# Graph attention layer: the edges' node numbers kept on chip and spread over the partitions by TensorE

## The chip, the cores and the metric

The kernel runs on one core of a Trainium2 chip. The metric is the device time of one execution in microseconds (us). All times here come from runs on the chip, or from the trace of one profiled execution.

## The reference

One layer of a graph network with a layer norm ahead of it and a residual around it: 12,500 nodes of 128 features, 200,000 edges, sorted by the node `dst` that they end in. What is computed, shortened:

```python
h = relu(layernorm(x))                       # (12500, 128)
Q, K = h @ W_Q.T, h @ W_K.T
score = einsum('md,md->m', Q[dst], K[src]) / sqrt(128) * exp(-edge_weight)   # per edge
# per node dst: keep the 16 best scores, softmax over them -> alpha (0 for the other edges)
agg = segment_sum(alpha[:, None] * (h[src] @ W_msg.T), dst)
out = x + relu(h @ W_self.T + agg)
```

## The kernel before

**Tiling.** The edges are cut into chunks of 128 (one edge per partition) and the chunks into G = 112 groups of GC = 14. Since edges are sorted, a group's edges end in some 112 consecutive nodes; a group also looks at the first chunk of the next (NJ = 15 chunks), so that its nodes are complete. W_Q and W_K are folded into one matrix `a_qk`, so the score of an edge is (h[dst] a_qk) . h[src].

**Prologue.** x is loaded in seven pieces on SyncE's (SP's) queue, normalised on ScalarE (`normed`, L214) and written to the table `h_tab` in device memory. `src`, `dst` and `edge_weight` are loaded as rows of 13 chunks (`load_rows`, on ScalarE's queue) and turned into columns by TensorE transposes (`to_columns`): the indices of the gathers (`idx_all`), each edge's rank within its node (`pos_all`), its decay (`dec_all`) and its node, from which `dlw` (the node's place relative to the group's first node) is made. `gather` (L172) fetches the rows of 128 edges with one indirect DMA, issued by GpSimd (POOL); a group has 14 of these. The first RAW = 4 groups are gathered straight from x, before `h_tab` is there, and normalised afterwards (`raw_stats`, `raw_normed`); groups 4 to 6 are gathered from `h_tab` all at once behind them. Their rows lie in `hs`, a ring of seven groups.

**The main loop** (the listing's `for i in range(-3, G + 6)`) is a software pipeline written out by hand: the order of the calls is each engine's order of instructions (`tc.manual_schedule()`), and one iteration holds stages of different groups. For a group, in the order of its data:

- `load_dst` brings `dst` of 15 x 128 edges, the same row to all 128 partitions, into `dstb` (960 KB over SP's queue). `far_of` (L522) takes the square of its distance from the partition's node in one ScalarE pass of 128x1920, `to_edges` (L527) makes a 0/1 matrix `to_e` (node by edge) of it. `places` (L533, L535) makes two small 0/1 tables.
- `q_to_edges` (L546), in four parts b = 0 to 3, spreads q of the nodes over the edges with `to_e`: three bf16 products per chunk. `scores` (L556) multiplies with the gathered rows on VectorE (DVE).
- `scores_in_slots` (L564), `slots_by_node` (L569, L571: 30 products) and `slots_out`, `node_by_slots` bring the scores of a node together in 40 slots; `best` (L585 to L597) finds the 16 best on VectorE: `ell` is its first result, `km` its last. `sum_of_exps` (L602) is on ScalarE.
- `kept_to_edges` (L614, 15 products) brings the verdict back to the edges; `on_edges` (L620 to L627), `exps` (L631) and `weights` (L635, L636) make the weights `alz`.
- `sums` (L646), in two parts of seven and eight chunks, adds up the weighted rows in PSUM. `sums_out` (L651) writes them to `agn`, `sums_turned` (L654) transposes, `sums_turned_out` (L658) copies to `aggT`, `products` (L661, L662), `output` (L666) and `store` finish the group.

`let_go(g, k)`, called as `more(k)` at seven places of an iteration, copies two columns of indices (L472, on VectorE) and issues two gathers of a later group: POOL waits for the copy, and for the `hs` buffer of seven groups earlier to be free, which `sums` has read last. In one iteration the calls `more(0)` to `more(4)` and `more(5)`, `more(6)` belong to two groups.

PSUM has eight banks of 128 x 512 words; `bank(tag, bufs)` hands them out. The sums have one, tag `a`, with a single buffer:

```python
            if part == 0:
                T[g]["pa"] = bank("a", 1)
```

Of the kernel before, what the change touches and what calls it, by code (L numbers as in the profile page):

```python
# [41 lines left out]
RAW = 4  # L42
# [34 lines left out]
def gnn_layer(  # L77
# [38 lines left out]
    CPR = 13  # L116
# [4 lines left out]
    assert RR <= P and RR - RF <= 1  # L121
# [22 lines left out]
    nvec = const.tile([P, 1], F32, name="nvec")  # L144
    a_qk = const.tile([P, P], F32, name="a_qk")
# [8 lines left out]
    nb = const.tile([P, G], F32, name="nb")  # L154
# [79 lines left out]
    with tc.tile_pool(name="edges", bufs=1) as ep, ExitStack() as stage:  # L234
        prep = stage.enter_context(tc.tile_pool(name="prep", bufs=1))
        RL = HALO + RW

        src_r = ep.tile([RR, RL], I32, name="src_r")
        h0 = src_r.bitcast(F32)
        h1 = alz[0][0:RR, 0:RL]  # L240
        dst_all = alz[1][:, 0:CW]
        assert max(RL, CW) <= NJ * (WW + STEP)
        dst_r = ep.tile([RR, HALO + RW], I32, name="dst_r")
# [24 lines left out]
        nc.vector.memset(src_r, 0)  # L268
        load_rows(src_r, src)
        xs, t = [], 0  # L270
        for i, n in enumerate(sizes):
# [12 lines left out]
        nc.vector.memset(ew_r, 0.0)  # L284
# [10 lines left out]
        nc.vector.memset(dst_all[:, RR * CPR:CW], float(1 << 21))  # L295
# [13 lines left out]
        def finish(i):  # L309
            t0, n, xg = xs[i]  # L310
            normed(xg, n, *stat[i])
            if i == 1:
                for t, w in zip(ws, (w_q, w_k, w_self, w_msg)):
                    nc.scalar.dma_start(t, w)
                nc.scalar.dma_start(b_i[:, 1:G],
                                    bass.AP(dst.tensor, dst.offset + EG - 1, [[EG, 1], [EG, G - 1]]))

# [10 lines left out]
            if i == 1:  # L328
                load_dst(0)
# [6 lines left out]
        for g in range(RAW, min(7, G)):  # L336
            gather_at_once(g, h_tab)
# [592 lines left out]
```

## Time and profile before

| | us |
|---|---|
| time, median of 9 runs | 2692.22 |
| lowest and highest | 2687.59 and 2698.76 |
| the profiled execution's own time | 2688.1 |
| its span in the trace | 2686.3 |
| first gather of the main loop | 213.63 |
| end of the last gather | 2610.16 |

The mean granted TensorE clock of the profiled execution is 0.691. In the lines of the profile, PE is TensorE's products, PEld its weight loads, DVE VectorE, ACT ScalarE, POOL GpSimd, SP SyncE; L172 is a line of the kernel. A line of the timeline has start and duration in us, then engine, line, operation, output <- inputs, the count, and in brackets the idle time before it and what ended it ("remote": a signal of another engine that the trace can't place; "issue": nothing that the trace shows). A line of the waits has the time waited in all, the number of waits and the longest. Matmuls are pipelined, and their ends in the trace are modelled.

### The profile page before, as it was taken

The numbers are of one execution on the slowest core, as the hardware profiler recorded it, in microseconds if no ns is written. First come the engines' busy times: TensorE is split into PE (matmuls) and PEld (weight loads), VectorE is DVE, ScalarE is ACT, GpSimd is POOL, SyncE is SP. The second block draws the span as 40 slices with busy tenths as digits, with TensorE's granted clock in tenths as the row PEclk, the third lists the DMA queues.
The fourth block names the chain that finished last, engine by engine and source line by source line (L and its number), as shares of the span: only waits on it lengthen the run. The fifth ranks groups of instructions, "written<-read, shape, count | busy, mean of one in ns | idle before, by whom it ended". The sixth has DMA issues, their size and how long they took to land. (4 is left out here: it accounts for less than half of the span.)

```text
span 2686.3 us, 43581 instructions
## 1 busy us (share of the span) xinstructions
PE 1740.9 (65%) x14574; PEld 1484.2 (55%) x14575; DVE 1475.9 (55%) x7420; ACT 648.4 (24%) x1306; POOL 1526.1 (57%) x1578
## 2 busy tenths in 40 slices
PE   0236666666767666766676766766776677766676
PEld 0125555555555655655555655555565566565555
DVE  5547555555555555555555555555555555555555
ACT  5532122222222222222222222222222222222221
POOL 4725555555555665555555555555566655555550
PEclk9657676666666667667666666666667766666668
DMA  8412322333333233322232332332323232222320
GB/s 223 151 57 91 93 94 92 94 94 94 94 94 95 95 95 94 94 90 86 90 94 91 95 94 93 94 94 94 95 95 95 94 94 92 87 89 92 93 81 8
DMA packets 117572, 253.17 MB, mean 94 GB/s; under 512 B 32798, under 2 KB 76065, under 8 KB 116576
## 3 DMA queue, kind: packets, MB, share of 16 engines
q1 hardware_dynamic: 66104, 144.92, 15.6%
q0 software_dynamic: 50144, 102.74, 14.3%
q10 hardware_dynamic: 1094, 2.69, 0.5%
q8 instruction: 115, 1.88, 0.3%
q14 instruction: 115, 0.94, 0.1%
HBM read 236.40 MB, written 14.40 MB: 93 GB/s over the span
## 5 line engine op out<-in xcount | busy, mean ns | idle before, releaser
L172 POOL DMA_INDIRECT hs<-h_tab,ix x1465 | 1415.4, 966 | 1034.0 <-DVE prod L556 492.2
L646 PE MATMUL a<-hs,alz 128*128 128x128 f32 x3348 | 729.3, 384 | 98.3 <-issue 83.6
L646 PEld LDWEIGHTS a<-hs,alz 128*128 128x128 f32 x3348 | 664.3, 290 | 154.6 <-issue 122.9
L546 PE MATMUL q<-q,to_e 128*128 128x128 bf16 x5022 | 545.1, 259 | 281.5 <-issue 232.8
L546 PEld LDWEIGHTS <-to_e 128*128 128x128 bf16 x5022 | 417.1, 115 | 364.0 <-issue 353.3
L556 DVE SCALAR_TENSOR_TENSOR prod<-hs,dec_all,q 128x128 f32<-128x128 f32 x1674 | 483.6, 343 | 68.2 <-remote 31.3
L585 DVE TENSOR_SCALAR ell<-slots,e 128x40 f32<-128x40 f32 x112 | 27.9, 249 | 864.7 <-remote 820.6
L571 PE MATMUL e<-ow,sl 128*41 128x40 f32 x3348 | 248.2, 247 | 50.9 <-issue 46.1
L602 ACT ACTIVATE e<-v,km 128x16 f32<-128x16 f32 x112 | 34.4, 307 | 972.0 <-DVE km L594 957.1
L571 PEld LDWEIGHTS e<-ow,sl 128*41 128x41 f32 x3348 | 216.0, 162 | 74.1 <-issue 57.6
L651 ACT ACTIVATE agn<-a,rden 128x128 f32<-128x128 f32 x112 | 41.2, 368 | 777.8 <-remote 486.5
L654 PE MATMUL s<-ident,agn 128*128 128x128 f32 x112 | 39.1, 349 | 283.9 <-ACT up L631 89.8
L522 ACT ACTIVATE far<-dstb,nb 128x1920 bf16<-128x1920 int32 x112 | 212.9, 1901 | 0.0
L527 ACT ACTIVATE to_e<-far 128x1920 bf16<-128x1920 bf16 x112 | 201.1, 1796 | 0.0
L654 PEld LDWEIGHTS s<-ident,agn 128*128 128x128 f32 x112 | 17.1, 153 | 305.1 <-ACT agn L651 114.5
L556 DVE DVE_READ_ACCUMULATOR prod<-hs,dec_all,q 128x1 f32 x1674 | 137.5, 82 | 0.0
L472 DVE COPY ix<-idx_all 128x2 int32<-128x2 int32 (+1 forms) x733 | 130.6, 178 | 0.0
L614 PE MATMUL x<-km,to_e 128*128 128x43 bf16 x1674 | 78.8, 204 | 43.0 <-DVE km L597 34.0
L614 PEld LDWEIGHTS <-to_e 128*128 128x128 bf16 x1674 | 66.0, 112 | 69.9 <-DVE km L597 61.7
L666 DVE SCALAR_TENSOR_TENSOR o<-s,x_t 128x128 f32<-128x128 f32 x112 | 32.5, 290 | 126.1 <-issue 119.1
L506 PE MATMUL s<-a_qk,hT 128*128 128x128 f32 x224 | 57.4, 339 | 66.8 <-issue 48.2
L564 DVE TENSOR_TENSOR sl<-po,s 128x600 f32<-128x600 f32 x112 | 87.7, 783 | 3.8
(166 smaller groups left out, 1643.3 us busy)
## 6 DMA issues: line engine op xcount, KB each, us to landing
dstb<-in_dst_dram SPq DMA_DIRECT2D x111, 960.0 KB
hs<-h_tab,ix POOLq DMA_INDIRECT x1465
h_r<-h_tab SPq DMA_DIRECT2D x112, 64.0 KB
x_t<-in_x_dram SPq DMA_DIRECT2D x108, 64.0 KB
out_dram<-o SPq DMA_DIRECT2D x108, 64.0 KB
xg<-in_x_dram SPq DMA_DIRECT2D x2, 1400.0 KB
h_tab<-xg SPq DMA_DIRECT2D x2, 1400.0 KB
xg<-in_x_dram SPq DMA_DIRECT2D x1, 1120.0 KB
```

The source lines that it names most:

```text
L172: nc.gpsimd.indirect_dma_start(out=T[g]["hs"][:, j, :], out_offset=None, in_=table[0:N, :], in_offset=bass.IndirectOffsetOnAxis(ap=index(j ...
L472: nc.vector.tensor_copy(ix[:, j0:j1], idx_all[:, GC * g + j0:GC * g + j1])
L506: nc.tensor.matmul(so[:, P:2 * P], lhsT=T[g]["hT"], rhs=a_qk, start=True, stop=True)
L522: nc.scalar.activation(T[g]["far"][:, 0:n], T[g]["dstb"][:, 0:n], AF.Square, bias=nb[:, g:g + 1])
L527: nc.scalar.activation(T[g]["to_e"][:, 0:n], T[g]["far"][:, 0:n], AF.Relu, bias=1.0, scale=-1.0)
L546: nc.tensor.matmul(pq[:, (j - j0) * P:(j - j0 + 1) * P], lhsT=T[g]["to_e"][:, j * P:(j + 1) * P], rhs=upper(T[g]["q"][:, k, :]), start=(k ...
L556: nc.vector.scalar_tensor_tensor(prod, rows_of(g, j), dec_all[:, c:c + 1], T[g]["pq", b][:, (j % 4) * P:(j % 4 + 1) * P], op0=OP.mult, op1 ...
L564: nc.vector.tensor_tensor(sl1[g % 2][:, 0:n, 0:KM], T[g]["po"][:, 0:n, :], bc(T[g]["s"][:, 0:n], KM), op=OP.mult)
L571: nc.tensor.matmul(et[0:KM + 1, STEP * j:STEP * j + WN], lhsT=sl1[g % 2][:, j, :], rhs=T[g]["ow"][:, j, :], start=False, stop=(j == n - 1))
L614: nc.tensor.matmul(px[:, j, 0:KM + 3], lhsT=T[g]["to_e"][:, j * P:(j + 1) * P], rhs=upper(T[g]["km"]), start=True, stop=True)
L646: nc.tensor.matmul(T[g]["pa"][:, 0:P], lhsT=alz[g % 2][:, WW * j + PRE:WW * j + PRE + P], rhs=rows_of(g, j), start=(j == 0), stop=(j == n ...
L654: nc.tensor.transpose(so[:, 2 * P:3 * P], T[g]["agn"], ident)
```

## The change

Rows now hold 14 chunks, one row per group (`CPR = GC`). A constant `rel` (bf16, 112 x 1920) holds for every group, on the group's own partition, the nodes of its 15 chunks minus the group's first node. The broadcast of `dst` (`load_dst`, `dstb`) goes. In its place `far_of(g, b)`, for b = 0 to 3, multiplies `rel` by a column of the identity, broadcast to 128 columns: a product that puts row g of 512 columns (384 in the last part) on all partitions, in the PSUM bank with tag `a`; ScalarE takes the Square from there, with the partition's number as bias. The four calls are put at four places of the iteration. `far` has two buffers instead of one. `dlw` is made by 15 such products with the identity, in place of the transposes of `dst` and three VectorE passes over 128x1680.

`src` is loaded first on SP's queue, ahead of x, and the weights, `dst` and `edge_weight` follow x on the same queue (ScalarE's before). RAW is 3 instead of 4. Groups 3 to 6 are gathered from `h_tab` by `let_go`: group 3 in seven steps between the VectorE instructions of the prologue, groups 4, 5 and 6 in iterations -1, 0 and 1 of the loop. The index copies have a ring of six buffers instead of four. The two `memset` of `alz` go from VectorE to GpSimd.

```diff
--- before.py
+++ after.py
@@ -39,7 +39,7 @@
-RAW = 4
+RAW = 3
@@ -113,12 +113,12 @@
-    CPR = 13
+    CPR = GC
     RW = CPR * P
     REM = M - RF * RW
-    assert RR <= P and RR - RF <= 1
+    assert RR == G and RR <= P and RF > 1 and (REM == 0 or REM >= P)
     CW = GC * (G + 1)
@@ -142,6 +142,9 @@
     nvec = const.tile([P, 1], F32, name="nvec")
+    minus = const.tile([P, 1], F32, name="minus")
+    rel = const.tile([RR, RW + P], BF16, name="rel")
     a_qk = const.tile([P, P], F32, name="a_qk")
...
@@ -176,14 +178,16 @@
-    def load_dst(g):
-        n = chunks[g] * P
-        lo = g * EG
-        T[g]["dstb"] = dstb = rows_pool.tile([P, NJ * P], I32, name="dstb", bufs=2)
-        hi = min(lo + n, M)
-        if hi < lo + n:
-            nc.vector.memset(dstb[:, hi - lo:n], 1 << 21)
-        nc.sync.dma_start(dstb[:, 0:hi - lo], dst[lo:hi].partition_broadcast(P))
+    def let_go(g, k):
+        j0, j1 = 2 * k, min(2 * k + 2, own[g])
+        if j0 >= j1:
+            return
+        if k == 0:
+            T[g]["ix"] = rows_pool.tile([P, GC], I32, name="ix", bufs=6)
+        ix = T[g]["ix"]
+        nc.vector.tensor_copy(ix[:, j0:j1], idx_all[:, GC * g + j0:GC * g + j1])
+        gather(g, j0, j1, lambda j: ix[:, j:j + 1])
...
@@ -248,10 +249,11 @@
         def load_rows(t, a):
-            if RF:
-                nc.scalar.dma_start(t[0:RF, 0:RW], a[0:RF * RW].rearrange("(p c) -> p c", c=RW))
+            nc.sync.dma_start(t[0:RF, 0:RW], a[0:RF * RW].rearrange("(p c) -> p c", c=RW))
             if REM:
-                nc.scalar.dma_start(t[RF:RF + 1, 0:REM], a[RF * RW:M].rearrange("(p c) -> p c", p=1))
+                nc.sync.dma_start(t[RF:RF + 1, 0:REM], a[RF * RW:M].rearrange("(p c) -> p c", p=1))
+                nc.sync.dma_start(t[RF:RF + 1, REM:RW], a[0:RW - REM].rearrange("(p c) -> p c", p=1))
...
@@ -274,14 +275,24 @@
             t += n
+        for t, w in zip(ws, (w_q, w_k, w_self, w_msg)):
+            nc.sync.dma_start(t, w)
+        nc.sync.dma_start(b_i[:, 1:G], bass.AP(dst.tensor, dst.offset + EG - 1, [[EG, 1], [EG, G - 1]]))
         make_identity(nc, ident)
-        nc.gpsimd.iota(dst_r, pattern=[[1, RL]], base=1 << 21, channel_multiplier=0)
+        nc.gpsimd.iota(dst_r, pattern=[[1, RL + P]], base=1 << 21, channel_multiplier=0)
         nc.gpsimd.memset(dst_r[0:1, 0:HALO], -1)
+        nc.sync.dma_start(dst_r[0:1, HALO:], dst[0:RW + P].rearrange("(p c) -> p c", p=1))
+        nc.sync.dma_start(dst_r[1:RF, :] if REM else dst_r[1:RF - 1, :],
+                          bass.AP(dst.tensor, dst.offset + RW - HALO, [[RW, RF - 1 if REM else RF - 2], [1, RL + P]]))
+        k = RF if REM else RF - 1
+        nc.sync.dma_start(dst_r[k:k + 1, 0:HALO + M - k * RW], dst[k * RW - HALO:M].rearrange("(p c) -> p c", p=1))
+        load_rows(ew_r, ew)
         nc.gpsimd.iota(slots, pattern=[[1, KM]], base=0, channel_multiplier=0,
                        allow_small_or_imprecise_dtypes=True)
-        nc.vector.memset(ew_r, 0.0)
+        for k in range(2):
+            nc.gpsimd.memset(alz[k], 0.0)
         nc.vector.memset(ones, 1.0)
...
@@ -309,32 +320,14 @@
             normed(xg, n, *stat[i])
-            if i == 1:
-                for t, w in zip(ws, (w_q, w_k, w_self, w_msg)):
-                    nc.scalar.dma_start(t, w)
-                nc.scalar.dma_start(b_i[:, 1:G],
-                                    bass.AP(dst.tensor, dst.offset + EG - 1, [[EG, 1], [EG, G - 1]]))
-                nc.scalar.dma_start(dst_r[0:1, HALO:], dst[0:RW].rearrange("(p c) -> p c", p=1))
-                if RF > 1:
-                    nc.scalar.dma_start(dst_r[1:RF, :], bass.AP(dst.tensor, dst.offset + RW - HALO,
-                                                                [[RW, RF - 1], [1, RL]]))
-                if REM:
-                    nc.scalar.dma_start(dst_r[RF:RF + 1, 0:HALO + REM],
-                                        dst[RF * RW - HALO:M].rearrange("(p c) -> p c", p=1))
-                load_rows(ew_r, ew)
             for a, b in cuts:
                 nc.sync.dma_start(by_part(h_tab)[a:b, t0:t0 + n, :], xg[a:b])
-            if i == 1:
-                load_dst(0)
                 finish(i)
-        for g in range(RAW, min(7, G)):
-            gather_at_once(g, h_tab)
@@ -354,6 +347,7 @@
         nc.vector.tensor_copy(row_i[:, 1, G - TAIL:G], row[:, 3, 0:TAIL])
+        let_go(RAW, 0)
         pb = bank("s", 1)
@@ -361,22 +355,29 @@
         nc.vector.tensor_copy(dst_f, dst_r)
+        let_go(RAW, 1)
+        nc.vector.tensor_scalar(rel, dst_f[:, HALO:], dst_f[:, HALO - 1:HALO], 1.0, op0=OP.subtract, op1=OP.subtract)
+        let_go(RAW, 2)
         nc.vector.memset(h0[:, 0:1], 0.0)
         nc.vector.tensor_tensor(h0[:, 1:RL], dst_f[:, 1:RL], dst_f[:, 0:RL - 1], op=OP.is_equal)
+        let_go(RAW, 3)
         nc.vector.tensor_tensor_scan(h1, h0, h0, 0.0, op0=OP.mult, op1=OP.add)
+        let_go(RAW, 4)
         bb = rows_pool.tile([P, 2, G], F32, name="bb")
         nc.vector.tensor_copy(bb, pb[:, 0:2 * G].rearrange("p (a g) -> p a g", a=2))
-        nc.vector.tensor_scalar(nb, bb[:, 0, :], nvec, -1.0, op0=OP.add, op1=OP.mult)
-        to_columns(dst_f, HALO, lambda at, p: nc.scalar.copy(at(dst_all), p))
+        for j0 in range(0, NJ, 4):
+            j1 = min(j0 + 4, NJ)
+            pt = bank("q", 3)
+            for j in range(j0, j1):
+                nc.tensor.matmul(pt[:, (j - j0) * RR:(j - j0 + 1) * RR], lhsT=rel[:, j * P:(j + 1) * P],
+                                 rhs=upper(ident[0:RR, 0:RR]), start=True, stop=True)
+            nc.vector.tensor_tensor(dlw.rearrange("e g j -> e j g")[:, j0:j1, :],
+                                    pt[:, 0:(j1 - j0) * RR].rearrange("e (j g) -> e j g", g=RR),
+                                    bc(w0[:, j0:j1], RR), op=OP.subtract)
         to_columns(h1, HALO, lambda at, p: nc.scalar.copy(at(pos_all), p))
         to_columns(ew_r, 0, lambda at, p: nc.scalar.activation(at(dec_all), p, AF.Exp, scale=-1.0))
-        byg = dst_all.rearrange("e (g j) -> e g j", j=GC)
-        nc.vector.tensor_sub(dlw[:, :, 0:GC], byg[:, 0:G, :], bc(bb[:, 0, :], GC))
-        nc.vector.tensor_sub(dlw[:, :, GC], byg[:, 1:G + 1, 0], bb[:, 0, :])
-        nc.vector.tensor_tensor(dlw, dlw, bm(w0, G), op=OP.subtract)
-        for k in range(2):
-            nc.vector.memset(alz[k], 0.0)
+        let_go(RAW, 5)
         nc.vector.scalar_tensor_tensor(h0[:, HALO:RL], dst_f[:, HALO - 1:RL - 1], 0.0, dst_f[:, HALO:RL],
...
@@ -516,10 +507,16 @@
-        def far_of(g):
-            n = chunks[g] * P
-            T[g]["far"] = win.tile([P, NJ * P], BF16, name="far", bufs=1)
-            nc.scalar.activation(T[g]["far"][:, 0:n], T[g]["dstb"][:, 0:n], AF.Square, bias=nb[:, g:g + 1])
+        def far_of(g, b):
+            n0, n1 = 4 * P * b, min(4 * P * (b + 1), chunks[g] * P)
+            if n0 >= n1:
+                return
+            if b == 0:
+                T[g]["far"] = win.tile([P, NJ * P], BF16, name="far")
+            pr = bank("a", 1)
+            nc.tensor.matmul(pr[:, 0:n1 - n0], lhsT=upper(ident[0:RR, g:g + 1]).to_broadcast([RR, P]),
+                             rhs=rel[:, n0:n1], start=True, stop=True)
+            nc.scalar.activation(T[g]["far"][:, n0:n1], pr[:, 0:n1 - n0], AF.Square, bias=minus)
@@ -683,8 +680,6 @@
             at(i + 3, load_nodes)
-            if i + 2 > 0:
-                at(i + 2, load_dst)
             if i == 8:
@@ -694,21 +689,29 @@
-                g, k = (i + 3, k + 2) if k < 5 else (i + 4, k - 5)
-                if 7 <= g < G:
+                if i in (-1, 0, 1):
+                    g = i + 5
+                else:
+                    g, k = (i + 3, k + 2) if k < 5 else (i + 4, k - 5)
+                    if g < 7:
+                        return
+                if i >= -1 and g < G:
                     let_go(g, k)
             at(i, q_to_edges, 0)
+            at(i + 1, far_of, 0)
             at(i - 5, output)
             at(i - 4, sums_turned)
+            at(i + 1, far_of, 1)
             at(i - 4, sums_turned_out)
             at(i, q_to_edges, 1)
-            at(i + 1, far_of)
+            at(i + 1, far_of, 2)
             at(i - 1, slots_by_node)
+            at(i + 1, far_of, 3)
             at(i + 1, places)
                 at(i + 1, raw_normed)
```

More of the change, by code (lines that the diff above doesn't have):

```diff
@@ L152, in gnn_layer @@
     dlw = const.tile([P, G, NJ], F32, name="dlw")
-    nb = const.tile([P, G], F32, name="nb")
     idxo = const.tile([P, TAIL], I32, name="idxo")
@@ L239, in gnn_layer @@
         h0 = src_r.bitcast(F32)
[L240 to L243, printed above, removed]
+        h1 = ep.tile([RR, RL], F32, name="h1")
+        dst_r = ep.tile([RR, RL + P], I32, name="dst_r")
         ew_r = ep.tile([RR, RW], F32, name="ew_r")
@@ L265, in to_columns @@
                     pt[:, 0:(j1 - j0) * RR].rearrange("e (j p) -> e j p", p=RR))
-        nc.vector.memset(src_r, 0)
         load_rows(src_r, src)
@@ L294, in gnn_layer @@
         nc.vector.memset(dec_all[:, RR * CPR:CW], 0.0)
-        nc.vector.memset(dst_all[:, RR * CPR:CW], float(1 << 21))
+        nc.vector.tensor_scalar(minus, nvec, -1.0, None, op0=OP.mult)
         for j in range(NJ):
@@ L390, in gnn_layer @@
         nc.vector.tensor_copy(badc, bad)
+        let_go(RAW, 6)
         t0 = ep.tile([P, TAIL], F32, name="t0")
@@ L462, in rows_of @@
             return T[g]["hs"][:, j, :] if j < GC else T[g + 1]["hs"][:, 0, :]
-        def let_go(g, k):
-            j0, j1 = 2 * k, min(2 * k + 2, own[g])
-            if j0 >= j1:
-                return
-            if k == 0:
-                T[g]["ix"] = win.tile([P, GC], I32, name="ix", bufs=4)
-            ix = T[g]["ix"]
-            nc.vector.tensor_copy(ix[:, j0:j1], idx_all[:, GC * g + j0:GC * g + j1])
-            gather(g, j0, j1, lambda j: ix[:, j:j + 1])
         def start_of(g, row, most):
```

## The prediction, made before the changed kernel was run

> **What bounds the kernel now.** I read the page's shares first, then the groups of instructions by form, the waits, and the timeline of two groups of edges.
>
> The page gives no engine more than 65% of the span:
>
> ```profile
> PE 1740.9 (65%) x14574; PEld 1484.2 (55%) x14575; DVE 1475.9 (55%) x7420; ACT 648.4 (24%) x1306; POOL 1526.1 (57%) x1578
> ...
> q1 hardware_dynamic: 66104, 144.92, 15.6%
> q0 software_dynamic: 50144, 102.74, 14.3%
> ```
>
> So the limit is a cycle of waits, not an engine's work. The waits name it:
>
> ```profile
> DVE ell L585 <- remote: 820.6, 96, 8.7
> POOL hs L172 <- DVE prod L556: 492.2, 208, 52.8
> ACT agn L651 <- remote: 486.5, 69, 7.3
> POOL hs L172 <- remote: 119.0, 71, 1.9
> ```
>
> GpSimd (POOL) issues one gather after another and stops twice per group. The timeline of one group:
>
> ```profile
> 1210.64 0.94 POOL L172 DMA_INDIRECT hs<-h_tab,ix  x1 [0.30 <-issue]
> 1215.67 0.95 POOL L172 DMA_INDIRECT hs<-h_tab,ix  x1 [4.09 <-DVE prod L556]
> 1221.94 0.94 POOL L172 DMA_INDIRECT hs<-h_tab,ix  x1 [0.30 <-issue]
> 1224.58 0.94 POOL L172 DMA_INDIRECT hs<-h_tab,ix  x1 [1.69 <-remote]
> ...
> 1206.01 0.26 PE L571 MATMUL e<-ow,sl 128*41 128x40 f32 x2 [0.45 <-issue]
> 1213.28 0.25 DVE L585 TENSOR_SCALAR ell<-slots,e 128x40 f32<-128x40 f32 x1 [8.70 <-remote]
> 1224.38 0.37 ACT L651 ACTIVATE agn<-a,rden 128x128 f32<-128x128 f32 x1 [7.05 <-remote]
> ```
>
> Eight gathers end at 1211.58. The last L571 matmul is recorded at 1206.01, yet the vector engine's `ell`, which needs it, starts only at 1213.28, 1.7 us after that burst's last gather. Then `best` (about 2 us) and an index copy let POOL go on at 1215.67. Six more gathers end at 1222.89; ScalarE's `agn` starts 1.5 us later, and then POOL. I call these two moments drain 1 and drain 2: what TensorE signals while gathers run reaches the other engines mostly when the burst has landed. So a group is 14 gathers x (0.966 + 0.30) = 17.7 us, plus pauses beyond 0.30 of about 3.8 and 1.4 us: 22.9 us. Without gathers the same group takes little more than half (columns: window, its length, busy time and count of PE, PEld, DVE, ACT, POOL, then granted clock, DMA share, GB/s):
>
> ```profile
> 1202.08:1224.96 22.88, 13.29 (x130) 10.98 (x131) 12.49 (x65) 5.10 (x10) 13.45 (x15) 0.85 0.30 93
> 2617.00:2629.50 12.50, 9.51 (x130) 8.82 (x131) 11.70 (x58) 5.21 (x10) 0.00 (x0) 1.00 0.02 7
> 213.60:2610.20 2396.60, 1641.59 (x13604) 1396.77 (x13602) 1315.20 (x6696) 534.51 (x1047) 1415.37 (x1465) 0.68 0.30 93
> ```
>
> Span: 213.6 (before the loop's first gather) + 2396.6 (1465 gathers, 104.6 groups of 14, 22.9 each) + 76.1 after the last = 2686.3, and 1.8 around it is the profiled 2688.1. The runs' median, 2692.2, is 4 us above it.
>
> **The change, part by part.**
>
> *Removed: the broadcast of dst.* 111 transfers of 960 KB, 544 KB for the last, are some 110 of q1's 144.9 MB. In the timeline they lie beside burst 1; burst 2 has none, and both issue a gather every 1.25 us. In the prologue's burst (108.6 to 160.8 us) only gathers moved, and ScalarE still waited:
>
> ```profile
> 111.62 0.41 PE L499 MATMUL s<-ident,h_r 128*128 128x128 f32 x1
> 159.06 0.27 ACT L503 COPY hT<-s 128x128 f32<-128x128 f32 x1 [41.91 <-remote]
> ```
>
> So the gathers, not this traffic, hold TensorE's signals back. Its worth in the loop: 0. (The Trainium skill, "DMA: Bandwidth & Descriptors", section "Issuing engines are not separate DMA queues", says all issuers share the same 16 engines and interleave. By that, the estimate is 110/144.9 of 15.6% of the span, some 317 us, at most.)
>
> *Prologue.* Sources land first, not behind x, so the first raw gather comes at about 11 us instead of 23.9. 42 raw gathers at 1.5 us (56 took 84.4 us) end near 74, before h_tab is written (81.7). The 42 gathers at once from h_tab go; group 3's 14 are let go from the vector engine's queue, 4 to 6 in iterations -1 to 1 at the loop's own pace. So TensorE isn't held for 42 us, and POOL's wait of 52.8 us before its first loop gather shrinks. With iteration -1 starting near 100 (group 0's first q matmul is at 107.8 now): 100 + three iterations with gathers (22.9) + 1.6 without (12.5) = 189. The early end: the three groups' 42 gathers alone take 42 x 1.27 = 53, which gives 173; all 4.6 at 22.9 give 205. Gain 24.6, between 9 and 41. Moved on queues: weights, dst and weights of edges go from ScalarE's queue to SP's, ahead of the h_tab writes; those wait for normalised rows (from 26 us) anyway, price 0 to 5. POOL's memsets of `alz` come before its first gather, which waits for the sources: 0 to 4, taken as 0. The 15 one-hot products that replace dst's transposes and three big vector passes: -3 to +2, taken as 0.
>
> *Added in the loop.* Per group, four one-hot matmuls of 512, 512, 512 and 384 columns and four Squares from PSUM. Rows of 128 bf16 columns start 0.056 us apart at full clock, 0.107 at half: 0.22 or 0.43 per matmul, under 1.7 in all, beside TensorE's 9.6 idle. Squares: now one of 1.91 (128x1920); in pieces about 0.62 each (a 128-column copy from PSUM, 0.27, plus 384 columns at L522's 1 ns each), 2.5 in all; ScalarE is 24% busy. Both lie in idle time; the work itself costs 0.
>
> *What isn't hidden: the order.* All four products and the sums of group i-3 use the one bank `a`. So each iteration has one closed chain: `agn` (bank free) -> product 0 -> Square 0 -> ... -> product 3 -> Square 3 -> sums part 0. Behind the products' waits stand, in TensorE's queue, L654, q's second part, L571 and q's third part with the sums; behind the Squares, on ScalarE, `aggT` and `q` (wanted an iteration later) and the exponentials of L602 (957 us of waiting in all: cover enough). Product 3 stands behind L571 in TensorE's queue, and L571's signal comes at drain 1. Product 3's likewise. So Square 3 starts at drain 1 at the earliest, and ends some 0.8 us later with its hand-over. Only then can the seven columns of sums part 0 start, of which now half are issued before drain 1. Behind them in TensorE's queue is L614, the kept slots to the edges. At a group whose clock is typical at that moment:
>
> ```profile
> 1488.31 0.25 DVE L585 TENSOR_SCALAR ell<-slots,e 128x40 f32<-128x40 f32 x1 [7.01 <-remote]
> 1490.42 0.73 PE L614 MATMUL x<-km,to_e 128*128 128x43 bf16 x15 [0.56 <-DVE km L597]
> 1490.71 0.95 POOL L172 DMA_INDIRECT hs<-h_tab,ix  x1 [3.66 <-DVE prod L556]
> 1492.47 3.22 PE L646 MATMUL a<-hs,alz 128*128 128x128 f32 x16
> ```
>
> and the granted clock around it (the third number from the end):
>
> ```profile
> 1487.90:1490.90 3.00, 2.23 (x20) 1.84 (x20) 2.38 (x18) 0.94 (x4) 0.19 (x1) 0.50 0.02 5
> ```
>
> L614 starts 2.1 us after `ell`, on `km`, and ends at +2.8, just after POOL's next burst starts (+2.4) and before its gathers land. After: 0.8 + 14 records x 0.20 (3.22/16) = +3.6 to 3.8. Burst 1 slowed TensorE's records about 1.5 us after its first gather (1201.68 to 1203.16), so at +3.9: L614, 15 products long, is caught. Its reader on the vector engine, L620 `on_edges`, runs at +6.2 now, in mid-burst. Caught, it waits for drain 2 (+11.1). Queued behind it on the vector engine is the index copy of `more(5)`, 2.1 us of `on_edges` later, plus 0.3 for the hand-over to POOL: the next burst starts at +13.6 instead of +11.3. Price 2.3 us a group. Bounds: 0 (L614 still in time) and +4 (product 0 also caught behind q's matmuls, Square 2 at drain 1, q's third part, queued behind product 3, late too). I take 2.3, since the clock row says 0.50.
>
> (The Trainium skill, "TensorE: Matmul & The Clock Gate", section "HAM oscillation — how this bites in real kernels", has the clock drop to half after idle windows, which short products separated by ScalarE's waits make likelier. It speaks against this change; warm, the sum would be 14 x 0.11 = 1.6, L614 at +2.4, in time.)
>
> Sum: 189 + 104.6 x 25.2 = 2636, + 78 (76 now, and one group's 2 more) = 2903; + 1.8 = 2905, and + 4 to the median: **2909**.
>
> **The rivals.**
> *Hidden (faster).* L614 is not caught, or Squares 0 to 2 and 3 slip through during burst 1, where TensorE does issue something each 0.7 us. Only the prologue counts: 189 + 2396.6 + 76.1 + 1.8 + 4 = 2667 (2651 to 2682 by its bounds). For it: L620 has 4.9 us of slack before drain 2, and the tail's records are 0.12 apart. Against it: clock 0.50 at drain 1. It decides at L614 ending before about +4. Chance 0.23.
> *Partly caught.* The lateness touches some groups only, 0.3 to 1.5 us on the mean: 2698 to 2824. Chance 0.10.
> *The broadcast did matter.* If it slowed TensorE, the two pauses (5.2 us a group) shrink by 1 to 4: 2250 to 2560. Against it: burst 2 and the prologue's burst. Chance 0.07.
> *Worse.* Product 1 or 2 is itself held to drain 1; then q's second part and L571's 30 products run after it and `ell` slips, by more than 4 us a group: over 3085. Chance 0.10.
>
> **How the numbers follow.** My forecast (1.5 to 4 us a group on 2667, so 2824 to 3085) has 0.50. The range, 2650 to 3085, reaches from the hidden case's early end to the forecast's late one; it leaves out the broadcast case and the worse one, 0.17. A measurement here tells about 0.2% (some 5 us) from no change; the runs spread over 0.4%. Faster: 0.21 of hidden + 0.07 = 0.28; same: 0.03 (hidden, with the prologue's gain lost, or little caught); slower 0.69.
>
> **What would show it.** Right: q1 near 35 MB; first loop gather near 189; `ell` still 1.7 us after burst 1; the last Square after drain 1, sums part 0 after it, L614 at +3.6 or later from `ell`; L620 waiting for drain 2; POOL's second pause 4 us instead of 1.7; period near 25.2. Wrong: L614 still bound by `km` at +2.1 (hidden), `ell` well before drain 1 (the broadcast), or L571's products recorded after it (worse).

## The result, and the profile after

The changed kernel takes 2700.24 us (median of 9 runs, 2698.49 to 2703.87), the kernel before 2691.51 (29 runs): ratio 1.0032, 95% interval 1.0019 to 1.0046. It is slower by 9 us where 217 were forecast; the sign and the range came out right, though not for the reason that the forecast gave, and the size did not. The profiled execution took 2701.8 us, 2700.0 of it span.

The line numbers after the change are lower by three from far_of on (L568 is the old L571, L582 L585, L611 L614, L617 L620, L643 L646, L648 L651); the gathers are at L174, the Squares at L519.

Cut at the loop's first gather and at the end of the last one (window, length, busy time and count of PE, PEld, DVE, ACT, POOL, then clock, DMA share, GB/s), the kernel before:

```profile
0.00:213.63 213.63, 50.67 (x436) 43.11 (x438) 112.18 (x489) 99.00 (x219) 106.00 (x109) 0.76 0.49 141
213.63:2610.16 2396.53, 1641.52 (x13604) 1396.69 (x13602) 1315.13 (x6696) 534.44 (x1046) 1415.37 (x1465) 0.68 0.30 93
2610.16:2686.30 76.14, 48.75 (x540) 44.35 (x539) 48.62 (x237) 14.91 (x43) 4.71 (x5) 0.86 0.03 9
```

and after:

```profile
0.00:207.25 207.25, 59.94 (x466) 46.30 (x468) 103.62 (x492) 95.62 (x216) 102.45 (x112) 0.79 0.41 112
207.25:2618.54 2411.29, 1636.80 (x13993) 1341.97 (x13993) 1314.20 (x6696) 610.38 (x1361) 1438.66 (x1465) 0.74 0.19 50
2618.54:2700.00 81.46, 55.03 (x569) 49.49 (x568) 48.64 (x236) 16.00 (x48) 4.21 (x4) 0.81 0.03 8
```

So the prologue gave 6.4 us (24.6 forecast), the loop cost 14.8 (240 forecast), and the tail 5.3 (2 forecast): 13.7 between the two profiles. The traffic did go; the loop's went from 93 to 50 GB/s, and the queue table has

```profile
q1 hardware_dynamic: 51027, 37.99, 5.0%
```

The waits of the changed kernel (us in all, times, longest):

```profile
DVE ell L582 <- remote: 751.7, 99, 7.7
ACT agn L648 <- remote: 707.8, 98, 7.3
ACT far L519 <- remote: 605.1, 102, 11.9
PEld a L643 <- ACT far L519: 427.8, 102, 5.1
POOL hs L174 <- DVE prod L553: 414.3, 208, 4.2
...
POOL hs L174 <- remote: 176.5, 95, 4.5
```

The third and fourth are the forecast chain: in 100 of 112 groups the last of the four Squares waited for a held signal, and the sums waited for that Square. POOL's two pauses are still the two drains: the first shorter by 0.2 us on the mean (3.62, 3.84 before), the second longer by 0.16 (2.00, 1.84). The timeline of one group:

```profile
1201.54 0.94 POOL L174 DMA_INDIRECT hs<-h_tab,ix  x1 [1.90 <-remote]
...
1204.04 1.44 POOL L174 DMA_INDIRECT hs<-h_tab,ix  x1 [0.30 <-issue]
...
1213.07 0.25 DVE L582 TENSOR_SCALAR ell<-slots,e 128x40 f32<-128x40 f32 x1 [7.61 <-remote]
1213.11 0.58 ACT L519 ACTIVATE far<-a,minus 128x384 bf16<-128x384 f32 x1 [5.83 <-remote]
1213.74 3.35 PE L643 MATMUL a<-hs,alz 128*128 128x128 f32 x14 [3.83 <-ACT far L519]
...
1215.46 0.94 POOL L174 DMA_INDIRECT hs<-h_tab,ix  x1 [3.75 <-DVE prod L553]
...
1216.89 0.76 PE L611 MATMUL x<-km,to_e 128*128 128x43 bf16 x15
...
1219.67 0.20 DVE L617 TENSOR_REDUCE up<-x 128x15 f32<-128x45 f32 x1 [0.33 <-PE a L643]
...
1224.30 0.37 ACT L648 ACTIVATE agn<-a,rden 128x128 f32<-128x128 f32 x1 [7.18 <-remote]
1224.49 0.94 POOL L174 DMA_INDIRECT hs<-h_tab,ix  x1 [1.81 <-remote]
```

The last Square starts at drain 1, the sums 0.67 after `ell` and not half before it, L611 at +3.82 instead of +2.1: the forecast within 0.15 us. But `on_edges` (L617) runs at +6.60, in mid-burst, not at +11. L611 was let through. In the kernel before, for the group whose `ell` is at 1213.28, `on_edges` was at +6.19:

```profile
1219.47 0.20 DVE L620 TENSOR_REDUCE up<-x 128x15 f32<-128x45 f32 x1
```

### The profile page after: what moved, and what is told of

The parts are those of the page before. It is cut to its first block, busy times and chain, and to the rows that moved or that the text cites. A ratio compares the mean times of both kernels' runs of the same rounds, so it can differ in the third digit from the quotient of the medians.

```text
span 2700.0 us, 44305 instructions
## 1 busy us (share of the span) xinstructions
PE 1751.8 (65%) x15026; PEld 1437.8 (53%) x15027; DVE 1466.5 (54%) x7422; ACT 722.0 (27%) x1622; POOL 1545.3 (57%) x1580
## 3 DMA queue, kind: packets, MB, share of 16 engines
q0 software_dynamic: 50144, 102.74, 14.5%
## 5 line engine op out<-in xcount | busy, mean ns | idle before, releaser
L174 POOL DMA_INDIRECT hs<-h_tab,ix x1521 | 1494.4, 983 | 1047.6 <-DVE prod L553 414.3
L643 PE MATMUL a<-hs,alz 128*128 128x128 f32 x3348 | 601.1, 351 | 413.2 <-ACT far L519 406.7
L643 PEld LDWEIGHTS a<-hs,alz 128*128 128x128 f32 x3348 | 557.7, 259 | 435.2 <-ACT far L519 427.8
L543 PEld LDWEIGHTS <-to_e 128*128 128x128 bf16 x5022 | 432.6, 119 | 393.9 <-issue 386.1
L519 ACT ACTIVATE far<-a,minus 128x512 bf16<-128x512 f32 (+1 forms) x447 | 294.9, 660 | 970.4 <-remote 605.1
L582 DVE TENSOR_SCALAR ell<-slots,e 128x40 f32<-128x40 f32 x112 | 27.9, 249 | 796.7 <-remote 751.7
L517 PE MATMUL a<-rel,ident 112*128 112x512 bf16 (+1 forms) x447 | 231.9, 519 | 73.7 <-ACT far L519 26.7
L648 ACT ACTIVATE agn<-a,rden 128x128 f32<-128x128 f32 x112 | 41.1, 367 | 782.3 <-remote 707.8
L568 PE MATMUL e<-ow,sl 128*41 128x40 f32 x3348 | 237.2, 257 | 0.2 <-DVE sl L561 0.2
L568 PEld LDWEIGHTS e<-ow,sl 128*41 128x41 f32 x3348 | 222.1, 175 | 15.0 <-DVE sl L561 0.4
L189 DVE COPY ix<-idx_all 128x2 int32<-128x2 int32 x761 | 135.4, 179 | 0.0
L651 PEld LDWEIGHTS s<-ident,agn 128*128 128x128 f32 x112 | 19.1, 170 | 170.5 <-DVE o L663 159.8
L651 PE MATMUL s<-ident,agn 128*128 128x128 f32 x112 | 48.6, 434 | 88.5 <-DVE o L663 81.7
L611 PEld LDWEIGHTS <-to_e 128*128 128x128 bf16 x1674 | 81.1, 115 | 16.6 <-issue 8.6
L633 DVE TENSOR_TENSOR alz<-ow,kept 128x600 f32<-128x600 f32 x112 | 87.5, 782 | 4.0
L561 DVE TENSOR_TENSOR sl<-po,s 128x600 f32<-128x600 f32 x112 | 87.6, 782 | 3.9
L624 DVE TENSOR_REDUCE kept<-mine 128x15 f32<-128x600 f32 x112 | 86.9, 776 | 3.8
L530 DVE TENSOR_TENSOR ow<-slots,dlw 128x600 f32<-128x600 f32 x112 | 86.7, 774 | 0.2 <-DMA h_r<-h_tab 0.2
```

What stands on the lines that cost most here:

```text
L174: nc.gpsimd.indirect_dma_start(out=T[g]["hs"][:, j, :], out_offset=None, in_=table[0:N, :], in_offset=bass.IndirectOffsetOnAxis(ap=index(j ...
L189: nc.vector.tensor_copy(ix[:, j0:j1], idx_all[:, GC * g + j0:GC * g + j1])
L517: nc.tensor.matmul(pr[:, 0:n1 - n0], lhsT=upper(ident[0:RR, g:g + 1]).to_broadcast([RR, P]), rhs=rel[:, n0:n1], start=True, stop=True)
L519: nc.scalar.activation(T[g]["far"][:, n0:n1], pr[:, 0:n1 - n0], AF.Square, bias=minus)
L543: nc.tensor.matmul(pq[:, (j - j0) * P:(j - j0 + 1) * P], lhsT=T[g]["to_e"][:, j * P:(j + 1) * P], rhs=upper(T[g]["q"][:, k, :]), start=(k ...
L561: nc.vector.tensor_tensor(sl1[g % 2][:, 0:n, 0:KM], T[g]["po"][:, 0:n, :], bc(T[g]["s"][:, 0:n], KM), op=OP.mult)
```

## The experiments

**Where they ran.** The runs fell on several chips, and these are of two kinds. On four (kernel before at 2091 to 2092 us) TensorE's signals are not held during the gathers; on two (2693 and 2716) they are, as in the result. Nothing in the kernels tells the chips apart, so each ratio is against the kernel before on the same chip. Each chip was seen for a short spell only, so whether it is the chip itself or its condition at the time is not shown.

| kernel | before there, us | ratio, interval |
|---|---|---|
| the change again | 2091.6 | 1.0010 (1.0001 to 1.0019) |
| the change, third | 2091.8 | 1.0008 (0.9999 to 1.0017) |
| last product ahead of L568, two chips | 2091.1, 2091.6 | 0.9997 (0.9987 to 1.0006), 0.9990 (0.9981 to 0.9999) |
| broadcast back, two chips | 2091.6, 2091.8 | 1.0009 (1.0000 to 1.0018), 1.0009 (0.9999 to 1.0018) |
| before with one broadcast | 2091.1 | 1.0003 (0.9993 to 1.0012) |
| L611 later, two chips | 2091.1, 2091.8 | 1.0010 (1.0001 to 1.0019), 1.0005 (0.9996 to 1.0013) |
| groups 4 to 6 by the loop's rule, two chips | 2091.6, 2091.8 | 1.0043 (1.0029 to 1.0056), 1.0043 (1.0031 to 1.0055) |
| broadcast back, L611 later, loop's rule | 2091.0 | 1.0043 (1.0025 to 1.0062) |
| groups 4 to 6 at once | 2716.5 | 1.0130 (1.0115 to 1.0144) |
| last product ahead, places cut | 2716.5 | 1.0094 (1.0076 to 1.0112) |
| broadcast back, L611 later, places cut | 2692.6 | 1.0543 (1.0524 to 1.0563) |
| the change, places cut | 2693.0 | 1.0033 (1.0021 to 1.0044) |
| before, places cut | 2693.0 | 0.9998 (0.9989 to 1.0007) |

**1. The two kernels again.**

> The changed kernel itself, once more, beside the kernel before on the same chip. In the two profiles at hand the third kernel (before with one broadcast) ran at 2092 us with POOL never pausing: 14 gathers x 1.285 = 18.0 us per group, while the profile of before, 2688 us, has 22.9 with two pauses. If the gathers hold TensorE's signals back here (kernel before near 2691): ratio 1.003 as in the result. If they don't (kernel before near 2091): POOL alone sets the period, 18.05 for both, and only the ends differ: first loop gather some 5 us earlier, tail within 1 us, ratio 0.997 to 1.000.

> The kernel before itself, for its profile. If TensorE's signals are held here: 2691 us, L571 to ell 7 us, the two pauses of 3.84 and 1.84 us. If not: about 2091 us, ell 0.04 us after L571's last product, no pause, 14 gathers x 1.285 = 18.0 us per group, one gather per group near 1.4 us.

> The changed kernel beside the kernel before, wherever this runs. Where TensorE's signals are held during the gathers (before at 2690 to 2720): ratio 1.003 as in the result, per group 23.05 to 23.3, third gather 1.41. Where they are not (before near 2091): ratio 1.001 again.

Measured: the change at 2093.2 and 2093.3 us (ratio 1.001, where 0.997 to 1.000 was expected first); the kernel before, on its turn, 2717.0 us with the pauses (3.98 and 1.95 us). In the change's timeline where signals are not held:

```profile
1204.21 2.32 PE L568 MATMUL e<-ow,sl 128*41 128x40 f32 x30
...
1205.41 0.94 POOL L174 DMA_INDIRECT hs<-h_tab,ix  x1 [0.30 <-issue]
1206.57 0.30 DVE L582 TENSOR_SCALAR ell<-slots,e 128x40 f32<-128x40 f32 x1 [2.72 <-PE e L568]
1206.66 0.95 POOL L174 DMA_INDIRECT hs<-h_tab,ix  x1 [0.30 <-issue]
```

`ell` follows L568's last product (1206.53) by 0.04 us, with gathers going on beside it; in the result's profile that distance was 4.7 us (median), in that of before 7.0. POOL never pauses: 18.05 us a group, and the same in the kernel before with one broadcast. Yet the gathers' packets come at the same times (medians: the first 1.65 us after the issue, the last 2.1 to 2.2, on both kinds). So the holding of TensorE's signals is not a property of the program or of the gathers' timing; its cause stays open.

**2. The one-bank chain.** The last product is put ahead of the 30 of L568:

```diff
+            at(i + 1, far_of, 3)
             at(i - 1, slots_by_node)
-            at(i + 1, far_of, 3)
```

> The last of the four one-hot products is put ahead of L568's 30 products (slots_by_node) in TensorE's queue; all else as after the change. Theory A (the change's loss in the loop comes from Square 3 being held to the first drain, so that the sums, L611 and q's fourth part are late): Square 3 runs during the first burst, sums part 0 starts before the drain, L611 is back at +2.1 us from ell, the third gather of a burst back from 1.41 to 1.15 us, the second pause from 2.00 to about 1.8; per group 23.05 - 0.26 - 0.16 = 22.63, time about 2656 (ratio to before 0.987). Rival B (the added products and Squares cost by themselves, wherever they stand): per group stays 23.05, time 2700. Rival C (the wait on Square 2, now ahead of L568, delays ell): more than 2700.

> The last one-hot product ahead of L568, once more. With TensorE held back (before near 2691): Theory A, per group 22.63, ratio 0.987; Rival B (the added work costs wherever it stands), 1.003; Rival C (ell delayed), more. Not held back (before near 2091): POOL sets the period, ratio 1.000 again.

Measured: within 0.1% of the kernel before, twice, where POOL alone sets the period (2089.5 us beside the change's 2093.2 on the chip that ran both); A, B and C are not told apart there. Experiment 6 has this order on the other kind.

**3. The broadcast.** Put back into the change (a tile that nothing reads), and left out of the kernel before:

```diff
...
+            if i + 2 > 0:
+                at(i + 2, load_dst)          # in the change: into an unused tile
```
```diff
-            if i + 2 > 0:
-                at(i + 2, load_dst)          # in the kernel before: T[0]["dstb"] for all groups
```

> The change, with the broadcast of dst loaded again, 960 KB per group on SP's queue at its old place, into a tile that nothing reads. With TensorE held back (before near 2691): Theory A (the broadcast delayed the landing of the first burst by some 0.3 us), first pause 3.62 to 3.84, per group 23.27, ratio 1.012; rival (traffic worth 0), 1.003. Not held back: POOL sets the period, 0 against the change.

> The change, with the broadcast of dst loaded again into a tile that nothing reads. Held (before at 2690 to 2720): Theory A (the broadcast delayed the landing of the first burst), first drain 0.3 us later after the burst's last gather, first pause 0.2 us longer, ratio 0.008 above that of the change; rival (the prediction's, traffic worth 0): the same as the change within 0.002. Not held: 0 against the change, as measured.

> The kernel before, with the broadcast of dst loaded for group 0 alone; all groups' far is made from that one tile, so 111 loads of dst and the right to_e of the other groups are left out. Theory A: the first pause goes from 3.84 to about 3.6 us, per group 22.90 - 0.22 = 22.68, time about 2668 (ratio 0.991). Rival (the prediction's: worth 0): 2692. The upper estimate from the queue's share, over 100 us less, would show as 2590 or less.

Measured: 0 in all three, where POOL alone sets the period. The question for the other kind is answered in 5.

**4. The start.** Groups 4 to 6 by the loop's general rule, and at once as before the change:

```diff
-                if i in (-1, 0, 1):
-                    g = i + 5
-                else:
-                    g, k = (i + 3, k + 2) if k < 5 else (i + 4, k - 5)
-                    if g < 7:
-                        return
-                if i >= -1 and g < G:
+                g, k = (i + 3, k + 2) if k < 5 else (i + 4, k - 5)
+                if 4 <= g < G:
                     let_go(g, k)
```
```diff
+        for g in range(4, 7):
+            gather_at_once(g, h_tab)         # behind let_go(RAW, 6); 7 <= g in more(k)
```

> The change, with groups 4 to 6 let go by the loop's general rule (two gathers of group 4 at the end of iteration 0, and so on), not in iterations -1 to 1. Theory (the 35 gathers of groups 3 to 5 that the changed prologue issues in one burst from 92 to 136 us hold TensorE until 144): group 4's first gather near 136 instead of 111, no pause of 31 us ahead of group 7, last gather 15 to 20 us earlier: ratio 0.006 below that of the change. Rival (the later start of 42 gathers costs POOL as much as the held TensorE did): within 0.002 of the change. Where POOL alone sets the period (before near 2091), the later start costs: 105 to 136 us for group 4's first gather, 15 to 20 us slower.

> The change, with groups 4 to 6 let go by the loop's general rule. Held: Theory (35 gathers in one burst from 92 to 136 us hold TensorE until 144), last gather 15 to 20 us earlier than the change's, ratio 0.006 below; rival (later start costs as much): within 0.002. Not held: 7 us slower than before, as measured.

> The change, with groups 4 to 6 gathered from h_tab in one go behind group 3, as before the change, and not from VectorE's queue in iterations -1 to 1. Theory (letting them go in the loop did not pace them: 35 gathers ran in one burst anyway): first gather of group 7 and time within 5 us of the change. Rival (pacing helped; the prediction's 24.6 us came from it): some 10 to 20 us slower than the change.

Measured: the general rule costs 0.43%, some 8 us (6 against the change, where 15 to 20 were forecast), where POOL sets the period; it was never measured where signals are held. At once, on a chip that holds them: the rival was right. The first gather of group 7 comes at 226.1 us, 207.2 with the change, and the first `ell` at 203.3 us, 184.4 with the change (188.6 and 191.6 in the two profiles of before). The change itself was not run on that chip, so the difference of the whole times is not read here. Yet pacing is only partial. In the changed kernel VectorE's index copies ran ahead of TensorE, POOL issued from 92.27 to 136.25 without a pause, and ScalarE shows how long TensorE was held; with all at once the same wait is 35.56 us long, to 168.52:

```profile
144.13 0.69 ACT L519 ACTIVATE far<-a,minus 128x512 bf16<-128x512 f32 x1 [11.89 <-remote]
```

**5. Held or slowed.** L611 is put behind q's fourth part. This ran alone, and together with the broadcast and the rule of 4, on chips that don't hold signals, and together with the broadcast and the cut of 6 on one that does; there the three edits are read in separate stretches of the trace:

```diff
-            at(i - 2, kept_to_edges)
 ...
             at(i, q_to_edges, 3)
+            at(i - 2, kept_to_edges)
```

> The change, with L611 (kept_to_edges) put behind the nine products of q's fourth part in TensorE's queue, so about 1 us later still, at +4.9 us from ell and wholly inside the second burst. Prediction's mechanism (what is caught is held to the second drain): on_edges waits to about +11.1, the index copy behind it to +13.4, per group some 2 us more, time about 2900. Theory A (caught products run slower, not held): on_edges at about +7.5 to +9, the copy still before the second drain, and q's fourth part is in time again: per group 22.8 to 23.1, time 2675 to 2705.

> The change, with L611 behind the nine products of q's fourth part. Held: the prediction's mechanism (caught in the second burst means held to the second drain), on_edges at +11 us from ell, the index copy at +13.4, per group some 2 us more, ratio 1.08; Theory A (caught products run slower, not held; q's fourth part in time again), on_edges at +7.5 to +9, per group within 0.3 us of the change. Not held: same as the change, as measured.

> Three edits in one kernel, read apart in its profile because they lie in different stretches: dst loaded again in the loop (read at the first drain), L611 behind the nine products of q's fourth part (read at on_edges), groups 4 to 6 let go by the loop's general rule (read before group 7's first gather). Only where TensorE's signals are held (before at 2690 to 2720). First drain: Theory A, ell 1.7 us after the burst's last gather, as before the change, and not 1.36; rival, 1.36. L611: the prediction's mechanism, on_edges at +11 us from ell and a second pause of some 4 us; Theory A, on_edges at +7 to +9, second pause under 2.2 us. Prologue: Theory, no pause of 31 us ahead of group 7; rival, as late as with the change. Not held: 7 us slower than before, no pauses.

> Three edits of the changed kernel, read apart: dst loaded again in the loop, L611 behind the nine products of q's fourth part, and the two passes of places cut into three of five chunks each. Where TensorE's signals are not held (before near 2091) the first two were measured at 1.0009 and 1.0005, so the ratio is that of the cut: Theory (a gather waits for the end of the pass it collides with), long gather from 1.35 to 1.0 to 1.15, per group 0.2 to 0.35 us less, ratio 0.983 to 0.991; rival (the collision is with SP's loads), 1.000. Where they are held (before 2690 to 2720): first drain, Theory A, ell 1.7 us after the burst's last gather and not 1.36, rival 1.36; L611, the prediction's mechanism, on_edges at +11 us from ell, Theory A +7 to +9 with a second pause under 2.2 us; long gather 1.41 to 1.15.

Measured, where signals are held: ratio 1.0543, the largest effect of all (alone, L611's move was not run there). The timeline of a caught group (L611 is L619 here, `on_edges` L625):

```profile
1200.37 0.25 DVE L590 TENSOR_SCALAR ell<-slots,e 128x40 f32<-128x40 f32 x1 [7.54 <-remote]
...
1202.77 0.94 POOL L174 DMA_INDIRECT hs<-h_tab,ix  x1 [4.04 <-DVE prod L561]
...
1204.90 0.53 PE L619 MATMUL x<-km,to_e 128*128 128x43 bf16 x15
...
1211.36 0.20 DVE L625 TENSOR_REDUCE up<-x 128x15 f32<-128x45 f32 x1 [4.72 <-remote]
...
1213.40 0.16 DVE L189 COPY ix<-idx_all 128x2 int32<-128x2 int32 x1
1214.32 0.94 POOL L174 DMA_INDIRECT hs<-h_tab,ix  x1 [4.33 <-issue]
```

L619 at +4.5 from `ell`, `on_edges` at +11.0, POOL at +13.95: the prediction's mechanism with its price. Sorted by `on_edges`, over the groups of the three kernels between 300 and 2600 us or so (count; mean second pause; mean time to the next `ell`; two outliers at +13 and +14.5 left out):

| on_edges from ell | before | change | broadcast back, L611 later, places cut |
|---|---|---|---|
| +6.2 to +6.7 | 94; 1.63; 22.8 | 88; 1.85; 23.0 | |
| +7.3 to +8.1 | 1; 1.91; 23.0 | 9; 1.9; 23.05 | 1; 1.5; 22.9 |
| +9.5 to +10.2 | 1; 2.87; 23.8 | 1; 2.85; 23.8 | 62; 2.9; 23.9 |
| +11 | 1; 4.28; 25.3 | | 34; 4.28; 25.3 |

In the second burst caught signals come through in steps of some 1.4 us (`on_edges` at +6.6, +8.1, +9.5, +10.9). Up to +8 the lateness is free: in the kernel with groups 4 to 6 at once, 78 of 99 groups have `on_edges` at +7.4 to +8.2, and their period is that of the 19 groups at +6.2 to +6.7 (23.28 and 23.31 us). At +9.5 it costs 0.95 us, at +11 2.4. So both were half right: not all that is caught is held, and what is held costs what was forecast. Theory A's bound on the pause (under 2.2) falls.

The first burst is different. Counted from the trace's semaphore events, from 1.4 us after a burst's first gather to its drain, 0.1 of TensorE's signals per group come through in the first burst of the kernel before, and 4.1 in the second. With the change it is 2.7 and 1.0, and those of the first burst come before +6 us, nearly all. Why the bursts differ is not shown.

The broadcast: with it back (and the passes of places cut), the first burst's start to `ell` is 11.43 us (median), with the change 11.54, before 11.54, so the traffic delays nothing. `ell` did come 1.67 us after the burst's last gather, as Theory A had it, but with the cut alone it does so too (1.65, see 6); Theory A's reading of the shorter first pause falls.

**6. The long gather.** One gather per group takes 1.41 us with the change and 1.15 before. Of the 100 gathers of the change after which the second pass of places begins within 0.2 to 0.75 us, all but one are long (over 1.05 us). The passes cut into three:

```diff
-            nc.vector.tensor_tensor(T[g]["ow"][:, 0:n, :], bm(slots, n), bc(dlw[:, g, 0:n], WN), op=OP.is_equal)
+            cut = [(a, min(a + 5, n)) for a in range(0, n, 5)]
+            for a, b in cut:
+                nc.vector.tensor_tensor(T[g]["ow"][:, a:b, :], bm(slots, b - a), bc(dlw[:, g, a:b], WN), op=OP.is_equal)
```

and `po` likewise.

> The change, with the last one-hot product ahead of L568, and the two VectorE passes of places (128x600 each) cut into three of five chunks each. One gather per group takes 1.3 to 1.45 us instead of 0.95, and in 77 to 99 of 100 of these the second pass of places began 0.3 to 0.7 us after it. Theory (a gather's writing waits for the end of that one pass): the long gather falls to 1.0 to 1.15 us, per group 0.2 to 0.35 us less; POOL-bound 18.05 to 17.8, ratio 0.985 to 0.99. Rival (the stretch comes from SP's loads of h_r and x_t, issued at the same moment): stays at 1.3 to 1.4, ratio 0.999.

> The change, with the two passes of places cut into three of five chunks each, and nothing else. In the profile of the kernel with three edits no gather was long any more (0.06 per group over 1.05 us, 1.02 with the change). Theory (the long gather costs its 0.4 to 0.45 us in full): where TensorE's signals are held (before at 2690 to 2720), per group 23.0 to 22.55, ratio 0.985 to 0.990; where not (before near 2091), per group 18.05 to 17.65, ratio 0.980 to 0.985. Rival (the pauses take the gain back, since both end at a drain that TensorE's work sets): held 1.000 to 1.003; not held, 0.980 to 0.985 all the same.

> The kernel before, with the same cut of places. Its long gather is 1.15 us where the signals are held and 1.4 where not. Theory: held, 0.2 per group less, ratio 0.991 to 0.993; not held, 0.4 per group less, ratio 0.980 to 0.985. Rival (the pauses take it back): held 1.000.

Measured: in the change the third gather of a burst fell from 1.43 to 1.01 us (medians) and the fourth rose from 0.94 to 1.10, so the long one did wait for that pass. But the time did not move: 1.0033 with the cut, 1.0032 without. The rival of the second text (the pauses take the gain back) was right: the mean first pause went from 3.62 to 3.89 us. In the kernel before, the long gather begins 0.44 us after the second pass, not ahead of it, and stayed at 1.15 us with the cut; its 0.9998 tells nothing here. The burst's timeline with the cut, in the change:

```profile
1200.30 0.95 POOL L174 DMA_INDIRECT hs<-h_tab,ix  x1 [1.88 <-remote]
...
1209.28 0.95 POOL L174 DMA_INDIRECT hs<-h_tab,ix  x1 [0.30 <-issue]
...
1211.87 0.25 DVE L585 TENSOR_SCALAR ell<-slots,e 128x40 f32<-128x40 f32 x1 [7.40 <-PE q L546]
```

From the burst's start to `ell` it is 11.57 us, where the group shown above had, with the long gather, 11.53 (1201.54 to 1213.07). Over all groups the medians are 11.54 (before), 11.54 (change), 11.58 (cut), though the last issue ends at 9.90, 10.17 and 9.93. Nor does `ell` follow the packets closely: the burst's last one has landed at 11.13, 11.42 and 11.10 us (same order). So POOL's issuing doesn't set drain 1, which comes some 11.5 us after the burst's first gather in all three; what does set it is not shown. That is also why the first pause was shorter with the change: the longer gather filled it. With the last product also ahead of L568 the ratio was 1.0094 on its chip: the first burst's start to `ell` 11.73 in the median, but 12.39 at the 95th percentile (11.72 before there), since Square 2 is then itself sometimes held and L568 behind it. Theory C, in part of the groups. Square 3 itself was freed, as Theory A had it: it starts 3.2 us ahead of `ell` there (median), 0.03 after it in the change. On a chip that doesn't hold signals, where the largest gain was forecast (ratio 0.980 to 0.985), the cut was not run, and no version here is faster than the kernel before by more than 0.1%.

## Why the prediction was wrong

**The term that was mis-sized** is L611's catch, 2.3 us x 104.6 groups = 240 us. Every step ahead of it came true: product 3 behind L568, Square 3 at drain 1, the sums at +0.67, L611 at +3.8 in the median, the clock 0.50 there (window 1213.74 to 1217.09). The step that failed is "caught, it waits for drain 2". It took the second burst to do what the first does: the slow stretch was to begin at +3.9 and to hold everything to +11.1. In the trace of the change L611's signal comes at +6.6 in most groups and +8 in seven, and VectorE has slack up to about +8.5 (POOL goes on 2.95 us after a late `on_edges`, and at +11.46 anyway, when drain 2 frees its buffer). The price of 2.3 is right for a group that is held all the way (2.4 in experiment 5), but for that L611 has to come a microsecond later still, and even then 34 of 97 groups were held so long. The profile of before would have told: signals come through its second burst, and it has one group at +9.5 and one at +11, beside one at +8.1 that cost 0.2.

**What the loop did lose** (read from the traces, not tested). Drain 2 itself opens at the same moment: the first of TensorE's signals in the run that ends with the sums comes 8.51 us after the second burst's start in both profiles. But `agn` needs the last of the sums' signals, and they come 0.043 us apart. Before, 5 signals were still in that run ahead of `agn`, since the sums stood over 1 us earlier (their second part at +4.1 from `ell`, now +5.3, medians); with the change 9: `agn` 0.19 and 0.36 us after the opening. That is 0.17 us a group, x 104.6 = 18 us, against 14.8 measured in the loop. It holds in the other profiles too (before with the cut: 5 signals, 0.19; change with the cut: 9, 0.36). No experiment took only this away.

**The prologue** gave 6.4 and not 24.6 us. Two terms failed. Being first on SP's queue did not bring the sources at once: VectorE's cast of them starts at 17.07 us instead of 19.82, and the first raw gather at 21.1, not 11. And "at the loop's own pace" failed: 35 gathers in one burst held TensorE to 144 us.

**The tail** cost 5.3 us, not 2: without gathers the four products and Squares on one bank seem to be a chain of their own (no run took them away). From `ell` to `ell` the first three groups there take 14.3, 14.2 and 14.3 us, before 12.6, 12.6 and 13.9. It was costed for the loop alone.

**Right:** the broadcast's 0 and ScalarE's Squares (0.69 and 0.58 us each; busy 27%). What the moves between queues cost was not measured apart. *The broadcast did matter* and *worse* are out; *hidden* was nearest in mechanism, but most of its prologue gain did not come. The time lies in the stretch of *partly caught* (2698 to 2824) by luck: that sum counts the prologue's 24.6 us as gained and adds a lateness of 0.3 us or more a group. The sign, too, is that of the forecast by other terms: the loop's 14.8 and the tail's 5.3 us outweigh the prologue's 6.4.

The clock rose, from 0.68 to 0.74 in the loop, and was 0.50 for the sums after drain 1 in both (median of the groups). (The Trainium skill, "TensorE: Matmul & The Clock Gate", section "HAM oscillation — how this bites in real kernels", tells of a kernel whose clock went back to half whenever the wait between two short runs of products grew too long. The prediction read it as speaking against the change; but the mean clock rose, and the 0.50 after drain 1 stood before the change too, so no run here shows the change lowering the clock.)

## What to carry to other kernels

A late link costs nothing until it passes the slack of what it feeds: find the next thing that its reader would wait for anyway, and price the lateness beyond that, from the few groups of the old trace in which the link was already late. What a signal meets in one stretch (here the first burst) need not hold in the next: look at each. When several edits each promise microseconds at the bursts' ends, ask what sets the end: here a burst ended a fixed time after its start, so neither some 107 MB less traffic nor 0.24 us less issuing moved it. And see whether a cycle bound by signals is bound so on every chip; here it was not.

## What was not expected of the hardware

The same program takes 2091 us on some chips and 2691 to 2717 on others, with the same packets; on the former TensorE's slot products reach `ell` in 0.04 us during gathers, on the latter 4.7 (change) or 7.0 us (before) later, when the burst is through. Where signals are held, those caught in the second burst of the kernel before come mostly 1.4 us apart, and 0.043 us apart after it; in its first burst almost none comes until the drain. A gather issued just ahead of one VectorE pass (128x600, is_equal of two f32 operands in SBUF) took 1.41 us instead of 0.95; passes of the same size with mult did not lengthen it (97 gathers ahead of L561 and 97 ahead of L633 in the change, none over 1.05 us).
